# Feed-forward order by hand or by the scheduler: a two-layer sequence kernel on one Trainium2 core

## The chip, the cores and the metric

The kernel runs on one core of one Trainium2 chip. The metric is the device time of one execution in microseconds. The kernel before took 5533.02 us (median of three runs, 5531.48 to 5550.13). A core has five engines that run side by side, each through its own queue of instructions: TensorE (PE in the profile, with its weight loads as PEld), VectorE (DVE), ScalarE (ACT), GpSimd (POOL) and SyncE (SP), which here only issues DMA transfers. The kernel is written in a tile language: the program allocates tiles from pools, and a scheduler orders the instructions of each engine and sets the waits when the program is built. The order is therefore fixed before the kernel runs.

## The reference

There are two layers over x of shape (4 batches, T = 512, 128, 64), with D = 128 x 64 = 8192 features per time step. All is fp32. Cut to what matters:

```python
# layer 0
xn = layernorm(x)                                  # over D
k, v, r = xn @ Wk, xn @ Wv, sigmoid(xn @ Wr)       # D -> 64
states = scan(s = decay * s + k*v)                 # over T
x = x + (r * states) @ Wo                          # 64 -> D
x = x + gelu(conv3(layernorm(x), freq_W))          # 3 taps along the 128, 64 -> 64 channels
to = layernorm(depthwise_causal_conv3(layernorm(x)))   # 3 taps along T
x = x + to
x = x + gelu(x @ ffn_W1) @ ffn_W2                  # 64 -> 256 -> 64, for each of the 128
# layer 1
trend = moving_average(x, 25)                      # along T
x = trend + irfft(W @ rfft(x - trend)[:128])       # 128 modes, one complex 128 x 128 matrix per channel
```

## The kernel before

In layer 0 the 8192 features lie on the partitions: 64 chunks of 128 features by 512 time steps, worked on in 32 pairs of chunks (NPR = 32, NCH = 64). For each batch a generator `front` makes the first half (projections, scan, attention, convolution along the 128) and writes x2 to DRAM; a generator `back` makes the second half (norm and time convolution in a first pass, residual and feed-forward in a second). The next batch's `front` is woven into this batch's `back`: each `yield` gives a weight, and the loop at the end advances the two in proportion. Small pools decide what can lie ahead: the PSUM pools have one buffer each, the SBUF pools two or three.

The convolution part of `front` (one step for each pair of chunks):

```python
        def attend(i):
            xp = load_x(i)
            at = two(ps_a, "a")
            for j in range(2):
                js = slice(j * S, (j + 1) * S)
                nc.tensor.matmul(at[:, j, :], lhsT=wo_sb[js, i, :], rhs=rst[js, :], start=True, stop=True)   # L382
            x1 = x1s[i] = two(fr, "x1")
            nc.vector.tensor_tensor(x1, at, xp, ALU.add)
            z = zs[i] = two(fr, "z")
            # ... z[j] = x1[j] * gain * rstd, on VectorE (L388), for j in 0, 1

        def convolve(i):
            cv = two(ps_c, "c")
            # L395: two matmuls with one row of weights (-mean * rstd times the gains through the convolution)
            # L401, L405: up to four 64 x 64 matmuls with the neighbours
            # L408: two 128 x 128 matmuls
            for j in range(2):
                c = 2 * i + j
                nc.scalar.activation(cv[:, j, :], cv[:, j, :], AF.Gelu_apprx_tanh, bias=cb[:, c : c + 1])
            x2 = two(bk, "x2")
            nc.vector.tensor_tensor(x2, cv, x1s.pop(i), ALU.add)
            nc.gpsimd.dma_start(x2d[b][2 * i : 2 * i + 2].rearrange("c p t -> p c t"), x2)
            sq2 = two(bk, "sq")
            nc.scalar.activation(sq2, x2, AF.Square)
            return x2, sq2
        # ... one step later add_up (L206): four matmuls with 32 columns of ones sum x2 and x2*x2,
        #     each into its own 32 rows of one PSUM bank
```

The projections of `front` (four 128 x 128 matmuls, L279, for each pair of chunks; weights `wq` and inputs `xp` are streamed, `wq` with two buffers) and the first pass of `back` (VectorE: two products, four taps; ScalarE: two scalings, a square; a store of `to`; then L206 sums) are not touched. Below is the second pass of `back`, which is:

```python
        def residual(i):
            x2 = fetch("kx", x2d, i)
            to = fetch("kt", tod, i)
            d = two(bk, "kd")
            nc.vector.tensor_tensor(d, to, pair_of(rb), ALU.mult)
            nc.vector.tensor_tensor(d, d, pair_of(mb), ALU.subtract)
            x3 = two(bk, "k3")
            for j in range(2):
                c = slice(2 * i + j, 2 * i + j + 1)
                nc.scalar.activation(d[:, j, :], d[:, j, :], AF.Identity, bias=vec[:, B4, c], scale=vec[:, G4, c])
            nc.vector.tensor_tensor(x3, d, x2, ALU.add)
            return x3

        def widen(c, m):
            x3 = x3s[c // 2][:, c % 2, :]
            pm = two(ps_m, "m")
            for h in range(2):
                hs = slice(h * H, (h + 1) * H)
                nc.tensor.matmul(
                    pm[:, h, :], lhsT=w1_sb[hs, m * P : (m + 1) * P], rhs=x3[hs, :], start=True, stop=True
                )
            mid = mids[c, m] = bk.tile([P, 2, SL], F32, tag="mid", name="mid", bufs=3)
            nc.scalar.activation(mid, pm, AF.Gelu_apprx_tanh, bias=fb1_sb[:, m : m + 1])

        def narrow(c):
            pa = ps_p.tile([P, SL], F32, tag="p", name="pa")
            for m in range(2):
                mid = mids.pop((c, m))
                for h in range(2):
                    nc.tensor.matmul(
                        pa[h * H : (h + 1) * H, :], lhsT=w2_sb[:, m, :], rhs=mid[:, h, :],
                        start=(m == 0), stop=(m == 1),
                    )
            x4t = x4s[c] = bk.tile([P, SL], F32, tag="x4t", name="x4t")
            nc.vector.scalar_tensor_tensor(x4t, pa, fb2_sb, x3s[c // 2][:, c % 2, :], ALU.add, ALU.add)
            if c % 2:
                x3s.pop(c // 2)

        def store(c):
            x4t = x4s.pop(c)
            pt = ps_p.tile([P, NT, P], F32, tag="p", name="pt")
            for t in range(NT):
                nc.tensor.transpose(pt[:, t, :], x4t[:, t * P : (t + 1) * P], ident)
            s = c // 4
            if c % 4 == 0:
                obs[s] = bk.tile([P, NT, SL], F32, tag="ob", name="ob")
            nc.scalar.copy(obs[s][:, :, c % 4 * P : (c % 4 + 1) * P], pt)
            if c % 4 == 3:
                nc.gpsimd.dma_start(
                    x4[b][:, s * SL : (s + 1) * SL].rearrange("(t p) d -> p t d", p=P), obs.pop(s)
                )

        yield 3.0
        for c in range(NCH + 1):
            if c < NCH:
                widen(c, 0)
            if c % 2 == 0 and c // 2 + 1 < NPR:
                x3s[c // 2 + 1] = residual(c // 2 + 1)
            if c > 0:
                narrow(c - 1)
            yield BACK
            if c < NCH:
                widen(c, 1)
            if c > 0:
                store(c - 1)
            yield BACK
```

The loop that weaves the two halves, with TensorE's order set by hand (it follows the program text instead of the scheduler's choice):

```python
    whole_front = 3.5 * NPR + 12.0 + 6.0 * NPR + 6.0
    whole_back = 5.0 * (NPR + 1) + 6.0 + 2.0 * BACK * (NCH + 1)
    with tc.manual_schedule(engines={nc.tensor.engine}):
        for _ in front(0):
            pass
        for b in range(B):
            second = back(b)
            first = front(b + 1) if b + 1 < B else iter(())
            ahead = 0.0
            for weight in second:
                ahead -= weight / whole_back
                while ahead < 0.0:
                    weight = next(first, None)
                    if weight is None:
                        break
                    ahead += weight / whole_front
            for _ in first:
                pass
```

Layer 1 follows when layer 0 is done: it takes all PSUM banks, and its order is the scheduler's in both kernels.

Of the kernel before, what the change touches and what calls it, by code (L numbers as in the profile page):

```python
# [10 lines left out]
F32 = mybir.dt.float32  # L11
AF = mybir.ActivationFunctionType
ALU = mybir.AluOpType
# [3 lines left out]
P = 128  # L17
T = 512
NF = 128
H = 64  # L20
D = NF * H
NCH = D // P
SL = 512
NS = D // SL
NPR = NCH // 2
NT = T // P
# [44 lines left out]
def layer0(ctx, tc, dram, x, xt, vecs, wkvr, wo, wdec, wconv, fbias, w1, fb1, w2, fb2, x4):  # L71


    nc = tc.nc
    B = x.shape[0]
# [8 lines left out]
    bk = ctx.enter_context(tc.tile_pool(name="bk", bufs=2))  # L84
# [5 lines left out]
    ps_m = ctx.enter_context(tc.tile_pool(name="ps_m", bufs=1, space=PSUM))  # L90
    ps_p = ctx.enter_context(tc.tile_pool(name="ps_p", bufs=1, space=PSUM))

    def two(pool, tag):
        return pool.tile([P, 2, SL], F32, tag=tag, name=tag)
# [16 lines left out]
    def load(name, src):  # L111
        t = const.tile(list(src.shape), F32, name=name)
        nc.scalar.dma_start(t, src)
        return t
# [6 lines left out]
    w1_sb = load("w1_sb", w1)  # L121
    fb1_sb = load("fb1_sb", fb1)
    w2_sb = load("w2_sb", w2)
    fb2_sb = load("fb2_sb", fb2)
# [76 lines left out]
    def add_up(st, i, pair, squares, first, last):  # L201

        for j in range(2):
            for k, src in ((0, pair), (1, squares)):
                q = 2 * j + k
                nc.tensor.matmul(  # L206
                    st[32 * q : 32 * q + 32, :], lhsT=ones, rhs=src[:, j, :],
                    start=first, stop=last,
                )
# [15 lines left out]
    def moments(mean, square, tag):  # L225

        var, rs, mrs = cols(f"var{tag}"), cols(f"rs{tag}"), cols(f"mrs{tag}")
        nc.vector.tensor_tensor(var, mean, mean, ALU.mult)
        nc.vector.tensor_tensor(var, square, var, ALU.subtract)
        rsqrt(rs, var)  # L230
        nc.vector.tensor_tensor(mrs, mean, rs, ALU.mult)
        return rs, mrs
# [9 lines left out]
    def pair_of(row):  # L242
        return row.unsqueeze(1).to_broadcast([P, 2, SL])
# [189 lines left out]
        carried[b] = rows(lambda: two(ps_c, "c"), *moments(mean3, sq3, 3), "rm3")  # L433

    carried = {}
    BACK = 0.2

    def back(b):

        rb, mb = carried.pop(b)  # L440

        def fetch(tag, src, i):
            t = two(bk, tag)
            nc.sync.dma_start(t, src[b][2 * i : 2 * i + 2].rearrange("c p t -> p c t"))
            return t


        st = ps_p.tile([P, SL], F32, tag="p", name="st4")
        waiting = None
        for i in range(NPR + 1):  # L450
            if i < NPR:
                x2 = fetch("kx", x2d, i)
                xr = two(bk, "kd")
                nc.vector.tensor_tensor(xr, x2, pair_of(rb), ALU.mult)
                xh = bk.tile([P, 2, SL + 2], F32, tag="kh", name="xh")
                nc.gpsimd.memset(xh[:, :, 0:2], 0.0)
                nc.vector.tensor_tensor(xh[:, :, 2:], xr, pair_of(mb), ALU.subtract)
                to = two(bk, "k3")
                for j in range(2):
                    c = slice(2 * i + j, 2 * i + j + 1)  # L460
                    nc.scalar.activation(  # L461
                        to[:, j, :], xh[:, j, 2:], AF.Identity, bias=tb_all[:, c], scale=vec[:, W2, c]
                    )
                    for k, w in ((1, W1), (0, W0)):
                        nc.vector.scalar_tensor_tensor(  # L465
                            to[:, j, :], xh[:, j, k : SL + k], vec[:, w, c], to[:, j, :], ALU.mult, ALU.add
                        )
                cc = slice(2 * i, 2 * i + 2)
                nc.vector.tensor_tensor(to[:, :, 0:2], to[:, :, 0:2], fix[:, cc, :], ALU.add)
                nc.gpsimd.dma_start(tod[b][cc].rearrange("c p t -> p c t"), to)  # L470
                sq = two(bk, "sq")
                nc.scalar.activation(sq, to, AF.Square)
            if waiting is not None:
                n, *pair = waiting
                add_up(st, n, *pair, n == 0, n == NPR - 1)
            waiting = (i, to, sq)
            yield 5.0
        mean, sq = finish(st, lambda: two(ps_m, "m"), 4)
        rs, mrs = moments(mean, sq, 4)
        rb, mb = rows(lambda: two(ps_m, "m"), rs, mrs, "rm4")  # L480
# [14 lines that stand above are left out]
            return x3  # L495

        x3s = {0: residual(0)}
        mids, x4s, obs = {}, {}, {}

        def widen(c, m):  # L500
            x3 = x3s[c // 2][:, c % 2, :]
            pm = two(ps_m, "m")
            for h in range(2):
                hs = slice(h * H, (h + 1) * H)
                nc.tensor.matmul(  # L505
                    pm[:, h, :], lhsT=w1_sb[hs, m * P : (m + 1) * P], rhs=x3[hs, :], start=True, stop=True
                )
            mid = mids[c, m] = bk.tile([P, 2, SL], F32, tag="mid", name="mid", bufs=3)
            nc.scalar.activation(mid, pm, AF.Gelu_apprx_tanh, bias=fb1_sb[:, m : m + 1])  # L509

        def narrow(c):
            pa = ps_p.tile([P, SL], F32, tag="p", name="pa")
            for m in range(2):
                mid = mids.pop((c, m))
                for h in range(2):
                    nc.tensor.matmul(  # L516
                        pa[h * H : (h + 1) * H, :], lhsT=w2_sb[:, m, :], rhs=mid[:, h, :],
                        start=(m == 0), stop=(m == 1),
                    )
            x4t = x4s[c] = bk.tile([P, SL], F32, tag="x4t", name="x4t")  # L520
            nc.vector.scalar_tensor_tensor(x4t, pa, fb2_sb, x3s[c // 2][:, c % 2, :], ALU.add, ALU.add)  # L521
            if c % 2:
                x3s.pop(c // 2)

        def store(c):
            x4t = x4s.pop(c)
            pt = ps_p.tile([P, NT, P], F32, tag="p", name="pt")
            for t in range(NT):
                nc.tensor.transpose(pt[:, t, :], x4t[:, t * P : (t + 1) * P], ident)
            s = c // 4  # L530
            if c % 4 == 0:
                obs[s] = bk.tile([P, NT, SL], F32, tag="ob", name="ob")
            nc.scalar.copy(obs[s][:, :, c % 4 * P : (c % 4 + 1) * P], pt)  # L533
            if c % 4 == 3:
                nc.gpsimd.dma_start(
                    x4[b][:, s * SL : (s + 1) * SL].rearrange("(t p) d -> p t d", p=P), obs.pop(s)
                )

        yield 3.0
        for c in range(NCH + 1):  # L540
            if c < NCH:
                widen(c, 0)
            if c % 2 == 0 and c // 2 + 1 < NPR:
                x3s[c // 2 + 1] = residual(c // 2 + 1)
            if c > 0:
                narrow(c - 1)
            yield BACK
            if c < NCH:
                widen(c, 1)
            if c > 0:  # L550
                store(c - 1)
            yield BACK


    whole_front = 3.5 * NPR + 12.0 + 6.0 * NPR + 6.0
    whole_back = 5.0 * (NPR + 1) + 6.0 + 2.0 * BACK * (NCH + 1)
    with tc.manual_schedule(engines={nc.tensor.engine}):
        for _ in front(0):
            pass
        for b in range(B):  # L560
            second = back(b)
            first = front(b + 1) if b + 1 < B else iter(())
            ahead = 0.0
            for weight in second:
                ahead -= weight / whole_back
                while ahead < 0.0:
                    weight = next(first, None)
                    if weight is None:
                        break
                    ahead += weight / whole_front  # L570
            for _ in first:
                pass


@with_exitstack
# [184 lines left out]
```

## Time and profile before

| What | Value |
|---|---|
| time, median of three | 5533.02 us |
| span of the profiled execution | 5531.1 us |
| TensorE busy | 4819.8 us, 87% |
| VectorE busy | 2204.9 us, 40% |
| ScalarE busy | 1681.4 us, 30% |
| GpSimd busy | 338.4 us, 6% |
| DMA | 897.45 MB, mean 162 GB/s |

The profile is of one execution. For each group of instructions it gives the source line, the engine, the tiles written and read, their shapes, the count, the busy time and the mean of one, and then how long the engine stood idle just before them and what ended that wait. An fp32 matmul appears as two records. A window view gives the busy time of every engine in a stretch of the execution, and the clock that TensorE was granted (1.00 is full speed). The chain of waits follows the work back from the last instruction, at each step to what released it. "L505" is line 505 of the kernel before; in the changed kernel the same lines of layer 0's second half lie one to three lines elsewhere.

### The profile page before, as it was taken

The numbers are of one execution on the slowest core, as the hardware profiler recorded it, in microseconds if no ns is written. First come the engines' busy times: TensorE is split into PE (matmuls) and PEld (weight loads), VectorE is DVE, ScalarE is ACT, GpSimd is POOL, SyncE is SP. The second block draws the span as 40 slices with busy tenths as digits, with TensorE's granted clock in tenths as the row PEclk, the third lists the DMA queues.
The fourth block names the chain that finished last, engine by engine and source line by source line (L and its number), as shares of the span: only waits on it lengthen the run. The fifth ranks groups of instructions, "written<-read, shape, count | busy, mean of one in ns | idle before, by whom it ended". The sixth has DMA issues, their size and how long they took to land.

```text
span 5531.1 us, 43935 instructions
## 1 busy us (share of the span) xinstructions
PE 4819.8 (87%) x16675; PEld 2000.1 (36%) x16675; DVE 2204.9 (40%) x2781; ACT 1681.4 (30%) x2091; POOL 338.4 (6%) x622
## 2 busy tenths in 40 slices
PE   7788888888888888888888757788999999999999
PEld 3322332222332222332222202224844844754664
DVE  3485467544457544457544494430011111111110
ACT  0022234455324455424455455550000000000000
POOL 1100011000001000001100010000000000000000
PEclk9799999999989999999999968999999999999999
DMA  8795665434565334475433353435355345345434
GB/s 273 235 302 176 213 213 178 135 136 138 197 221 185 133 135 149 149 246 186 145 133 137 106 214 122 137 107 165 90 165 158 92 162 160 107 145 161 122 120 146
DMA packets 443830, 897.45 MB, mean 162 GB/s; under 512 B 26140, under 2 KB 92188, under 8 KB 443492
## 3 DMA queue, kind: packets, MB, share of 16 engines
q1 hardware_dynamic: 350976, 613.49, 35.1%
q0 software_dynamic: 56832, 209.74, 10.2%
q10 hardware_dynamic: 35812, 71.43, 3.4%
q8 instruction: 131, 2.15, 0.2%
q14 instruction: 79, 0.65, 0.0%
HBM read 617.70 MB, written 276.86 MB: 162 GB/s over the span
## 4 chain that ended last, share of the span: by engine, by line
PE 69%; ACT 10%; DVE 9%; DMA 8%; issue 2%; POOL 0%; SPq 0%; ACTq 0%; POOLq 0%; DVEq 0%
PE m L505 8%; PE bank L623 8%; PE bank L670 8%; PE pa L516 8%; ACT mid L509 6%; PE a L279 5%; PE st L206 4%; PE bank L642 4%; PE bank L639 4%; PE bank L668 4%; PE bank L667 4%; PE c L408 4%; PE c L401 4%; DMA wq<-wqd 3%; PE c L395 2%
## 5 line engine op out<-in xcount | busy, mean ns | idle before, releaser
L505 PE MATMUL m<-k,w_sb 64*128 64x512 f32 x2048 | 580.1, 643 | 287.6 <-ACT mid L509 279.6
L509 ACT ACTIVATE mid<-m,fb_sb 128x1024 f32<-128x1024 f32 x512 | 568.5, 1110 | 417.0 <-PE m L505 417.0
L279 PE MATMUL a<-xp,wq 128*128 128x512 f32 x1024 | 493.1, 632 | 33.2 <-DMA wq<-wqd 27.4
L516 PE MATMUL pa<-mid,w_sb 128*64 128x512 f32 x2048 | 497.7, 607 | 10.6 <-ACT ob L533 10.6
L521 DVE SCALAR_TENSOR_TENSOR x4t<-pa,fb_sb,k 128x512 f32<-128x512 f32 x256 | 192.2, 751 | 771.8 <-PE pa L516 771.6
L670 PE MATMUL bank<-yf,idft_sb 128*128 128x512 f32 x1024 | 481.4, 591 | 0.0
L623 PE MATMUL bank<-xin,dft_sb 128*128 128x512 f32 x1024 | 441.8, 594 | 16.7 <-DMA halo<-x 16.7
L465 DVE SCALAR_TENSOR_TENSOR k<-xh,vec,k 128x512 f32<-128x512 f32 x512 | 358.1, 747 | 182.8 <-ACT k L461 174.9
L605 DVE COPY ob<-bank 128x512 f32<-128x512 f32 x128 | 88.5, 692 | 789.8 <-PE bank L670 789.8
L206 PE MATMUL st<-x,ones 128*32 128x512 f32 x512 | 252.3, 645 | 142.1 <-DVE x L413 142.1
L505 PEld LDWEIGHTS m<-k,w_sb 64*128 64x128 f32 x2048 | 155.7, 185 | 574.9 <-ACT mid L509 536.0
L411 ACT ACTIVATE c<-c,cb 128x512 f32<-128x512 f32 x256 | 169.2, 661 | 616.0 <-PE c L408 612.0
L413 DVE TENSOR_TENSOR x<-c,x 128x1024 f32<-128x1024 f32 x128 | 156.5, 1223 | 439.4 <-ACT c L411 439.1
L603 ACT COPY ob<-bank 128x512 f32<-128x512 f32 x128 | 75.0, 586 | 804.8 <-PE bank L670 804.8
L206 PE MATMUL st<-sq,ones 128*32 128x512 f32 x1024 | 306.5, 678 | 4.9
L279 PEld LDWEIGHTS a<-xp,wq 128*128 128x128 f32 x1024 | 198.0, 201 | 304.4 <-issue 281.1
L642 PE MATMUL bank<-xf,w 128*128 128x128 f32 x1024 | 304.3, 397 | 0.0
L639 PE MATMUL bank<-xf,w 128*128 128x128 f32 x1024 | 304.1, 397 | 0.0
L623 PEld LDWEIGHTS bank<-xin,dft_sb 128*128 128x128 f32 x1024 | 195.1, 191 | 262.3 <-issue 262.3
L670 PEld LDWEIGHTS bank<-yf,idft_sb 128*128 128x128 f32 x1024 | 192.9, 188 | 246.9 <-issue 246.9
L493 ACT ACTIVATE kd<-kd,vec 128x512 f32<-128x512 f32 x256 | 203.8, 807 | 248.9 <-DVE kd L489 248.9
L461 ACT ACTIVATE k<-xh,tb_all,vec 128x512 f32<-128x512 f32 x256 | 194.0, 804 | 255.1 <-PE st L206 174.6
(155 smaller groups left out, 5836.5 us busy)
## 6 DMA issues: line engine op xcount, KB each, us to landing
xp<-in_xt SPq DMA_DIRECT2D x256, 512.0 KB
kx<-x SPq DMA_DIRECT2D x256, 512.0 KB
xin<-x SPq DMA_DIRECT2D x128, 1024.0 KB
xk<-in_x SPq DMA_DIRECT2D x64, 1024.0 KB
x<-x POOLq DMA_DIRECT2D x128, 512.0 KB, 3.6
to<-k POOLq DMA_DIRECT2D x128, 512.0 KB, 3.8
kt<-to SPq DMA_DIRECT2D x128, 512.0 KB
x<-ob POOLq DMA_DIRECT2D x64, 1024.0 KB, 7.8
```

The costliest lines, as they stand in the source:

```text
L206: nc.tensor.matmul(st[32 * q : 32 * q + 32, :], lhsT=ones, rhs=src[:, j, :], start=first, stop=last,)
L279: nc.tensor.matmul(pa[:, k, :], lhsT=wq[:, j, k * P : (k + 1) * P], rhs=xp[:, j, :], start=first and j == 0, stop=last and j == 1,)
L401: nc.tensor.matmul(cv[0:H, j, :], lhsT=wc_sb[H:P, P:], rhs=prev[H:P, :], start=False, stop=False)
L408: nc.tensor.matmul(cv[:, j, :], lhsT=wc_sb[:, 0:P], rhs=z[:, j, :], start=False, stop=True)
L465: nc.vector.scalar_tensor_tensor(to[:, j, :], xh[:, j, k : SL + k], vec[:, w, c], to[:, j, :], ALU.mult, ALU.add)
L505: nc.tensor.matmul(pm[:, h, :], lhsT=w1_sb[hs, m * P : (m + 1) * P], rhs=x3[hs, :], start=True, stop=True)
L509: nc.scalar.activation(mid, pm, AF.Gelu_apprx_tanh, bias=fb1_sb[:, m : m + 1])
L516: nc.tensor.matmul(pa[h * H : (h + 1) * H, :], lhsT=w2_sb[:, m, :], rhs=mid[:, h, :], start=(m == 0), stop=(m == 1),)
L623: nc.tensor.matmul(pf, lhsT=dft_sb[:, k, r, :], rhs=xin[:, k, :], start=(k == 0), stop=(k == NT - 1))
L639: nc.tensor.matmul(o, lhsT=w[:, j, r, :], rhs=xf[:, 0, :, c], start=True, stop=False)
L642: nc.tensor.matmul(o, lhsT=w[:, j, 2 if r == 0 else 0, :], rhs=xf[:, 1, :, c], start=False, stop=True,)
L670: nc.tensor.matmul(po, lhsT=idft_sb[:, r, kk], rhs=yff[:, r, c], start=False, stop=(r == 1))
```

## The change

The feed-forward pass is written as one plain loop, and TensorE's order is left to the scheduler. Three things go: the hand-set order of TensorE, the functions that let the widening of one chunk run ahead of the narrowing of the chunk before it, and the small weights (0.2) that placed most of the next batch's `front` beside the first pass of `back`. In their place stand weights of 2, 2, 2 and 1 for each chunk. No arithmetic changes, and the pools and the transfers stay as they are. The stated purpose is a first layer with features on the partitions throughout, streamed over pairs of chunks from DRAM to DRAM; both kernels have that, so what differs is only the order.

```diff
@@ -433,7 +433,6 @@
         carried[b] = rows(lambda: two(ps_c, "c"), *moments(mean3, sq3, 3), "rm3")
 
     carried = {}
-    BACK = 0.2
 
     def back(b):
 
@@ -495,81 +494,65 @@
             return x3
 
         x3s = {0: residual(0)}
-        mids, x4s, obs = {}, {}, {}
-
-        def widen(c, m):
+        ob = None
+        yield 3.0
+        for c in range(NCH):
             x3 = x3s[c // 2][:, c % 2, :]
-            pm = two(ps_m, "m")
-            for h in range(2):
-                hs = slice(h * H, (h + 1) * H)
-                nc.tensor.matmul(
-                    pm[:, h, :], lhsT=w1_sb[hs, m * P : (m + 1) * P], rhs=x3[hs, :], start=True, stop=True
-                )
-            mid = mids[c, m] = bk.tile([P, 2, SL], F32, tag="mid", name="mid", bufs=3)
-            nc.scalar.activation(mid, pm, AF.Gelu_apprx_tanh, bias=fb1_sb[:, m : m + 1])
-
-        def narrow(c):
+            mids = []
+            for m in range(2):
+                pm = two(ps_m, "m")
+                for h in range(2):
+                    hs = slice(h * H, (h + 1) * H)
+                    nc.tensor.matmul(
+                        pm[:, h, :], lhsT=w1_sb[hs, m * P : (m + 1) * P], rhs=x3[hs, :], start=True, stop=True
+                    )
+                mid = bk.tile([P, 2, SL], F32, tag="mid", name="mid", bufs=3)
+                nc.scalar.activation(mid, pm, AF.Gelu_apprx_tanh, bias=fb1_sb[:, m : m + 1])
+                mids.append(mid)
+                yield 2.0
+            if c % 2 == 0 and c // 2 + 1 < NPR:
+                x3s[c // 2 + 1] = residual(c // 2 + 1)
             pa = ps_p.tile([P, SL], F32, tag="p", name="pa")
             for m in range(2):
-                mid = mids.pop((c, m))
                 for h in range(2):
                     nc.tensor.matmul(
-                        pa[h * H : (h + 1) * H, :], lhsT=w2_sb[:, m, :], rhs=mid[:, h, :],
+                        pa[h * H : (h + 1) * H, :], lhsT=w2_sb[:, m, :], rhs=mids[m][:, h, :],
                         start=(m == 0), stop=(m == 1),
                     )
-            x4t = x4s[c] = bk.tile([P, SL], F32, tag="x4t", name="x4t")
-            nc.vector.scalar_tensor_tensor(x4t, pa, fb2_sb, x3s[c // 2][:, c % 2, :], ALU.add, ALU.add)
-            if c % 2:
-                x3s.pop(c // 2)
-
-        def store(c):
-            x4t = x4s.pop(c)
+            x4t = bk.tile([P, SL], F32, tag="x4t", name="x4t")
+            nc.vector.scalar_tensor_tensor(x4t, pa, fb2_sb, x3, ALU.add, ALU.add)
+            yield 2.0
             pt = ps_p.tile([P, NT, P], F32, tag="p", name="pt")
             for t in range(NT):
                 nc.tensor.transpose(pt[:, t, :], x4t[:, t * P : (t + 1) * P], ident)
-            s = c // 4
             if c % 4 == 0:
-                obs[s] = bk.tile([P, NT, SL], F32, tag="ob", name="ob")
-            nc.scalar.copy(obs[s][:, :, c % 4 * P : (c % 4 + 1) * P], pt)
+                ob = bk.tile([P, NT, SL], F32, tag="ob", name="ob")
+            nc.scalar.copy(ob[:, :, c % 4 * P : (c % 4 + 1) * P], pt)
             if c % 4 == 3:
-                nc.gpsimd.dma_start(
-                    x4[b][:, s * SL : (s + 1) * SL].rearrange("(t p) d -> p t d", p=P), obs.pop(s)
-                )
-
-        yield 3.0
-        for c in range(NCH + 1):
-            if c < NCH:
-                widen(c, 0)
-            if c % 2 == 0 and c // 2 + 1 < NPR:
-                x3s[c // 2 + 1] = residual(c // 2 + 1)
-            if c > 0:
-                narrow(c - 1)
-            yield BACK
-            if c < NCH:
-                widen(c, 1)
-            if c > 0:
-                store(c - 1)
-            yield BACK
+                s = c // 4
+                nc.gpsimd.dma_start(x4[b][:, s * SL : (s + 1) * SL].rearrange("(t p) d -> p t d", p=P), ob)
+            if c % 2:
+                x3s.pop(c // 2)
+            yield 1.0
 
 
     whole_front = 3.5 * NPR + 12.0 + 6.0 * NPR + 6.0
-    whole_back = 5.0 * (NPR + 1) + 6.0 + 2.0 * BACK * (NCH + 1)
-    with tc.manual_schedule(engines={nc.tensor.engine}):
-        for _ in front(0):
+    whole_back = 5.0 * (NPR + 1) + 6.0 + 7.0 * NCH
+    for _ in front(0):
+        pass
+    for b in range(B):
+        second = back(b)
+        first = front(b + 1) if b + 1 < B else iter(())
+        ahead = 0.0
+        for weight in second:
+            ahead -= weight / whole_back
+            while ahead < 0.0:
+                weight = next(first, None)
+                if weight is None:
+                    break
+                ahead += weight / whole_front
+        for _ in first:
             pass
-        for b in range(B):
-            second = back(b)
-            first = front(b + 1) if b + 1 < B else iter(())
-            ahead = 0.0
-            for weight in second:
-                ahead -= weight / whole_back
-                while ahead < 0.0:
-                    weight = next(first, None)
-                    if weight is None:
-                        break
-                    ahead += weight / whole_front
-            for _ in first:
-                pass
 
 
 @with_exitstack
```

## The prediction

> **What bounds the kernel now.** I read the page first (shares, slices, chain), then a table of windows by stage, then three short stretches of the timeline.
>
> ```profile
> PE 4819.8 (87%) x16675; PEld 2000.1 (36%) x16675; DVE 2204.9 (40%) x2781; ACT 1681.4 (30%) x2091; POOL 338.4 (6%) x622
> ...
> PE 69%; ACT 10%; DVE 9%; DMA 8%; issue 2%; POOL 0%; SPq 0%; ACTq 0%; POOLq 0%; DVEq 0%
> ...
> L505 PE MATMUL m<-k,w_sb 64*128 64x512 f32 x2048 | 580.1, 643 | 287.6 <-ACT mid L509 279.6
> L206 PE MATMUL st<-x,ones 128*32 128x512 f32 x512 | 252.3, 645 | 142.1 <-DVE x L413 142.1
> ```
>
> TensorE is busy 87% and holds 69% of the chain that ended last. Its 711 us of idle time have two large owners: the widening matmul (L505) waiting for GELU (L509), 280 us, and the sums (L206) waiting for VectorE. TensorE's order is just what the change leaves to the scheduler.
>
> ```profile
> 606.00:770.00 164.00, 144.29 (x424) 59.72 (x424) 99.56 (x138) 45.80 (x53) 17.00 (x37) 0.94 0.79 275
> 794.00:1013.00 219.00, 191.93 (x737) 48.23 (x734) 150.03 (x184) 83.95 (x107) 28.80 (x52) 0.98 0.51 168
> 1033.00:1455.00 422.00, 349.25 (x1493) 111.76 (x1491) 179.42 (x181) 232.77 (x275) 19.20 (x26) 1.00 0.37 128
> ...
> 3161.00:3338.00 177.00, 94.98 (x280) 16.25 (x280) 162.39 (x228) 83.91 (x98) 27.74 (x65) 0.68 0.56 201
> 3350.00:3750.00 400.00, 303.59 (x1280) 97.02 (x1278) 158.73 (x155) 215.39 (x252) 12.15 (x16) 0.97 0.37 123
> 3754.00:4195.00 441.00, 440.81 (x1273) 250.68 (x1274) 43.68 (x64) 36.92 (x63) 11.23 (x18) 1.00 0.44 138
> ```
>
> Columns: window, length, busy PE, PEld, DVE, ACT, POOL (instructions), PE clock, DMA share, GB/s. The kernel is front of batch 0 alone (0 to 606 us), three like periods of about 850 us (606 to 1455, 1455 to 2308, 2308 to 3161), batch 3's back half alone (3161 to 3750), and layer 1 (3754 to the end, four times 442 us, TensorE full). A period is a **first part** of 427 us (k/v/r projections, back's norm pass, 26 of the next batch's 32 convolution steps) and a **feed-forward part** of 422 us with only 6 steps in it. In the first row the DMA is 79% busy; in the fourth, VectorE 92%.
>
> ```profile
> 1057.92 1.13 PE L505 MATMUL m<-k,w_sb 64*128 64x512 f32 x4 [0.69 <-ACT mid L509]
> 1058.97 1.94 PE L516 MATMUL pa<-mid,w_sb 128*64 128x512 f32 x8
> 1060.84 1.13 PE L505 MATMUL m<-k,w_sb 64*128 64x512 f32 x4
> 1061.90 0.65 PE L529 MATMUL pt<-ident,x4t 128*128 128x128 f32 x4
> ...
> 852.19 1.05 PE L206 MATMUL st<-x,ones 128*32 128x512 f32 x2 [0.71 <-DVE x L413]
> 853.31 0.62 PE L206 MATMUL st<-sq,ones 128*32 128x512 f32 x1
> ...
> 854.30 1.13 PE L395 MATMUL c<-rm,cgr 1*128 1x512 f32 x4
> ```
>
> An fp32 matmul shows as two records. Start to start, a widening pair costs 1.06 us (1057.92 to 1058.97), the four narrowing matmuls 1.87 us, the four transposes about 0.75. The last three lines are what the change multiplies: one sum alone holds TensorE as long (1.05 us) as the other three together (853.31 to 854.30, 0.99 us), since those lie in different columns of the array and run at once.
>
> **What the Trainium skill says.** "TensorEngine Tiling (Array Packing)", Key Properties: "Changing tiling mode (not just tile) drains the TensorE", and tiles work in parallel. The trace agrees: four half-width sums take the time of one, and each change of line costs about 0.15 us over its streaming time (1.87 us for four slots of 0.43). "TensorE: Matmul & The Clock Gate", Step-by-step, says that matmuls stay in program order and only weight loads are pulled ahead; the L505 waits with ready work behind them agree. The same page, on the clock gate, says an idle TensorE is slowed; the clock of 0.68 in the norm pass alone against 1.00 in the feed-forward part agrees.
>
> **The change part by part.** The arithmetic is the same: 8852 TensorE instructions before and after, by the built programs, whose orders are fixed before any run. Front 0 and layer 1 keep their order but for details. Four things move.
>
> (1) *Weights of the interleave.* The feed-forward part weighs 7.0 x 64 = 448 instead of 0.2 x 130 = 26. So the projections now run with the norm pass alone, and all 32 convolution steps go into the feed-forward part.
>
> (2) *First part, new.* The norm pass alone took 177 us (row 3161:3338), VectorE-bound at 10.25 us per two steps (a chain of VectorE taps and the 5 us store of its result). Now 25 MB of projection loads lie beside it: two steps move 3.67 MB, which in 10.25 us would be 358 GB/s, where the stretch 606 to 770 sustained 275 at a share of 0.79. TensorE has 8 x 0.87 + 3.1 + switches, 10.3 us, as well. I take 12.5 us: 16 x 12.5 = 200, plus 12 to start, 212. The end of the sums, residual 0 and the state scan of the next batch now lie together: 26 us (before, 20 to 25 us each at 770 and 1013). First part: **238 us**, 189 less than 427.
>
> (3) *Feed-forward part, new.* TensorE's work with all groups whole: per chunk 2 x 1.06 + 1.87 + 0.75 = 4.74 us, x 64 = 303 (the trace has 303.6); per convolution step 0.98 (L382) + 1.05 (L395) + 1.86 (L401, L405) + 1.91 (L408) + 1.05 (L206) = 6.85, x 32 = 219; together 522. But the scheduler cuts groups up. I counted the stretches in the built order of this part: L395 stands alone 50 times (25 lost pairs), L382 24 times (12 pairs), the sums split 1 and 3 in 27 steps of 32, and 106 half-groups of narrowing. With each lone matmul at 1.0 to 1.05 us: widening 136, narrowing 125, transposes 46, L382 43, L395 57, L401/L405 62, L408 61, sums 60, in all 591. That is 69 us of lost packing. Next, one dense step laid out by hand: 18.5 us of TensorE, VectorE 9.1 (1.22 + 1.41 + 1.23 for the step, 3.68 + 1.50 for two chunks) and ScalarE 9.6. I find one stall of about 0.6 us per step, at the second widening pair, where GELU stands behind the convolution's two GELUs in ScalarE's queue. 32 x 0.6 = 19, plus some start: **615 us**, 193 more than 422.
>
> So a period goes from 849 to 853 us. Put in another way: TensorE's idle time falls from 129 (849 less 720 busy) to 92 us (68 in the first part, where its own work is 170, and 24 in the second), while its work grows from 720 to 761 (+69 for lost packing, less 27 since the 26 steps in the old first part already paid for the sum of x2 alone). Three periods: +12 us.
>
> (4) *Feed-forward of batch 3 alone.* Before, order by hand: widen, narrow the chunk before, widen, store. The trace repeats in 11.94 us per two chunks (L505 starts at 3501.35 and 3513.29). The new order is widen, transpose, widen, narrow *the same* chunk. Laid out with the same durations (first pair 1.06, GELU 1.11 with 0.18 ahead and 0.06 behind): odd chunk 5.75 us, because the second half of narrowing waits out the second GELU. In the even chunk two ScalarE scalings surround that GELU, and the first waits for VectorE (x4t, x3, two products: 4.7 us after narrowing ends), so it takes 7.6 us. 13.35 per two chunks against 11.94: 32 x 1.41 = **+45 us**.
>
> Sum: 5533 + 12 + 45 = 5590. I add 20, since the hand layout of (3) supposes that VectorE and ScalarE come in time everywhere: **5610 us**.
>
> **The rivals.** *Filling wins*: the convolution steps fill every GELU wait and lone matmuls overlap their neighbours on free rows or columns. For it: the 280 us of L505 waits and engines half empty in that part. Against: a narrowing or transposing neighbour takes all rows. If packing cost half of 69 us, a period is 35 us shorter, total 5505. *The in-order engines collide*: TensorE's finer interleave makes it wait on VectorE or ScalarE instructions stuck behind others, as ScalarE's L493 already does here. For it: two streams share single PSUM buffers. Against: the same schedule orders all engines. At 10% idle in that part a period is 45 us longer: 5745. *The DMA takes the first part*: the weight loads queue on SyncE behind loads that wait for VectorE. At 15 us per two steps, +40 a period, 5730; were the norm pass undisturbed, 35 less, 5505.
>
> **Range and chances.** Each rival is worth about 100 us either way, part (4) about 20. Low 5500, high 5730. The line at plus 2% is 5644, at minus 2% 5422. Faster 0.07, within 0.53, slower 0.40.
>
> **What would show it.** The first part (first projection to first widening matmul) 220 to 260 us with DMA share 0.8 or more; the feed-forward part 600 to 640 us with TensorE over 95% busy; L382 and L395 with a higher total busy time than now; the L505 waits on GELU cut to under 130 us, most of them in batch 3; that part 430 to 450 us from its first widening matmul to its last store, not 395. I am wrong if a period differs from 850 us by over 40, if the feed-forward part has TensorE under 90%, or if front 0 or layer 1 moves by over 10 us.

## The result and the profile after

| | before | after |
|---|---|---|
| time, median of four | 5532.33 us (5531.48 to 5550.13) | 5575.32 us (5570.81 to 5582.84) |
| ratio, 95% interval | 1 | 1.0071 [1.0048, 1.0095] |
| span of the profiled execution | 5531.1 us | 5571.3 us |

The changed kernel is 0.7% slower: 43 us by the medians, 40 us by the two profiled spans. The page of the changed kernel has these lines in place of those shown of before (shares by engine, the chain, two groups):

```profile
PE 5094.9 (91%) x16675; PEld 2025.8 (36%) x16675; DVE 2185.8 (39%) x2781; ACT 1687.9 (30%) x2091; POOL 337.3 (6%) x622
...
PE 35%; DVE 4%; ACT 2%; DMA 1%; issue 1%; SPq 0%; POOL 0%; ACTq 0%; DVEq 0%; POOLq 0%
...
L506 PE MATMUL m<-k,w_sb 64*128 64x512 f32 x2048 | 604.6, 649 | 85.5 <-ACT mid L510 78.0
L518 PE MATMUL pa<-mid,w_sb 128*64 128x512 f32 x2048 | 552.8, 623 | 71.5 <-ACT mid L510 71.5
```

With the same 16675 records TensorE is busy 275 us longer, and its idle time has fallen from 711 to 476 us. The wait of the widening matmul for GELU (L505 before, L506 now) went from 280 to 78 us, but the narrowing matmul (L518) now waits 72 us for the same GELU, almost all of it in batch 3 (67). The chain breaks off early in this trace (its shares sum to 43%), so I don't use it. The stages say more; the windows of the changed kernel (columns as before: window, length, busy PE, PEld, DVE, ACT, POOL, clock, DMA share, GB/s):

```profile
220.00:668.00 448.00, 378.88 (x948) 98.86 (x948) 238.30 (x339) 82.00 (x102) 27.33 (x38) 0.80 0.54 178
...
887.00:1501.00 614.00, 594.96 (x2184) 173.53 (x2184) 277.06 (x291) 290.45 (x350) 35.73 (x49) 0.98 0.39 132
1501.00:1695.00 194.00, 177.71 (x570) 57.44 (x566) 166.88 (x235) 86.74 (x102) 28.23 (x67) 0.99 0.88 314
1714.00:2327.00 613.00, 593.95 (x2178) 172.62 (x2178) 276.54 (x287) 290.31 (x350) 35.74 (x49) 0.98 0.39 132
...
3347.00:3790.00 443.00, 317.94 (x1276) 91.97 (x1276) 153.82 (x151) 213.37 (x250) 12.15 (x16) 0.97 0.32 108
```

The rows are the convolution steps of front 0, a feed-forward part, a first part, the next feed-forward part, and batch 3's feed-forward alone. The same row of before for front 0 is

```profile
220.00:604.00 384.00, 304.71 (x979) 86.29 (x978) 238.74 (x346) 83.09 (x103) 29.48 (x39) 0.89 0.65 214
```

A stage of sums ends here where TensorE starts on the matmuls (L217) that read the finished sums (L206). With these ends the 40 us split like this:

| Stage | before, us | after, us | difference |
|---|---|---|---|
| front 0 (start to the end of its sums) | 603.7 | 668.1 | +64.4 |
| three periods | 2554.5 | 2484.0 | -70.5 |
| norm pass of batch 3 | 176.9 | 175.0 | -1.9 |
| feed-forward of batch 3, to layer 1 | 419.1 | 466.8 | +47.7 |
| layer 1 | 1776.9 | 1777.4 | +0.5 |

So the small number hides three large ones. In a period (the second of the three) TensorE's busy time rose from 722 to 782 us and its idle time fell from 131 to 44; front 0 and the last batch's feed-forward gave more than that gain back.

### The profile page after: what moved, and what is told of

It reads as the page before. It is cut to its first block, busy times and chain, and to the rows that moved or that the text cites. A ratio compares the mean times of both kernels' runs of the same rounds, so it can differ in the third digit from the quotient of the medians.

```text
span 5571.3 us, 43812 instructions
## 1 busy us (share of the span) xinstructions
PE 5094.9 (91%) x16675; PEld 2025.8 (36%) x16675; DVE 2185.8 (39%) x2781; ACT 1687.9 (30%) x2091; POOL 337.3 (6%) x622
## 5 line engine op out<-in xcount | busy, mean ns | idle before, releaser
L506 PE MATMUL m<-k,w_sb 64*128 64x512 f32 x2048 | 604.6, 649 | 85.5 <-ACT mid L510 78.0
L518 PE MATMUL pa<-mid,w_sb 128*64 128x512 f32 x2048 | 552.8, 623 | 71.5 <-ACT mid L510 71.5
L279 PE MATMUL a<-xp,wq 128*128 128x512 f32 x1024 | 511.5, 634 | 34.5 <-DMA wq<-wqd 33.6
L206 PE MATMUL st<-x,ones 128*32 128x512 f32 x512 | 268.4, 639 | 59.5 <-DVE x L413 59.5
L206 PE MATMUL st<-k,ones 128*32 128x512 f32 x512 | 238.0, 699 | 91.6 <-DVE k L468 91.6
L506 PEld LDWEIGHTS m<-k,w_sb 64*128 64x128 f32 x2048 | 164.6, 187 | 421.0 <-issue 232.0
L206 PE MATMUL st<-sq,ones 128*32 128x512 f32 x1024 | 308.9, 682 | 1.3 <-ACT sq L471 0.4
L279 PEld LDWEIGHTS a<-xp,wq 128*128 128x128 f32 x1024 | 186.1, 197 | 331.8 <-issue 310.9
L401 PE MATMUL c<-z,wc_sb 64*64 64x512 f32 x504 | 288.8, 696 | 0.0
L405 PE MATMUL c<-z,wc_sb 64*64 64x512 f32 x504 | 288.2, 695 | 0.4 <-DVE z L388 0.3
```

What stands on the lines that cost most here:

```text
L206: nc.tensor.matmul(st[32 * q : 32 * q + 32, :], lhsT=ones, rhs=src[:, j, :], start=first, stop=last,)
L279: nc.tensor.matmul(pa[:, k, :], lhsT=wq[:, j, k * P : (k + 1) * P], rhs=xp[:, j, :], start=first and j == 0, stop=last and j == 1,)
L401: nc.tensor.matmul(cv[0:H, j, :], lhsT=wc_sb[H:P, P:], rhs=prev[H:P, :], start=False, stop=False)
L405: nc.tensor.matmul(cv[H:P, j, :], lhsT=wc_sb[0:H, P:], rhs=after[0:H, :], start=False, stop=False)
L506: nc.tensor.matmul(pm[:, h, :], lhsT=w1_sb[hs, m * P : (m + 1) * P], rhs=x3[hs, :], start=True, stop=True)
L518: nc.tensor.matmul(pa[h * H : (h + 1) * H, :], lhsT=w2_sb[:, m, :], rhs=mids[m][:, h, :], start=(m == 0), stop=(m == 1),)
```

## The experiments

The theory after the result had four parts. (a) Front 0 is longer because the scheduler breaks up packed groups of matmuls there, and the clock falls as a consequence. (b) The periods are shorter because the convolution steps are spread over the feed-forward part, not because of the scheduler's order. (c) That order costs about 69 us of lost packing per period. (d) Batch 3 is longer because each chunk's narrowing waits out its own GELU. The rivals: front 0 waits for transfers or VectorE; the scheduler's own interleave makes the gain; the DMA sets the length of a period; batch 3 lacks a PSUM buffer, whatever the order.

### Front 0 by hand, and with its pairs whole

Two kernels, each the changed one with an edit to front 0. The first sets TensorE's order there by hand again; the second leaves it to the scheduler but for one edge per step, so that a step's convolution is issued after the sums of the step before.

```diff
-    for _ in front(0):
-        pass
+    with tc.manual_schedule(engines={nc.tensor.engine}):
+        for _ in front(0):
+            pass
```

> The changed kernel with TensorE's program order kept in front 0 alone. Theory 1 (the 64 us that front 0 lost, 604 to 668 us, come from TensorE's order alone: the two one-row matmuls L395 apart, and the slower clock that follows): front 0 ends near 604 us, a convolution step takes 9.7 us again, total 5511 us (5500 to 5525). Rival (front 0 lost because VectorE's statistics L288 and the loads of xk stand elsewhere in the queues): front 0 stays above 640 us, total 5555 to 5575.

```diff
-                waiting = (i - 1, *convolve(i - 1))
+                if b == 0 and i > 1:
+                    with tc.issue_after(added[0].ins):      # added[0]: the last of the four sums
+                        waiting = (i - 1, *convolve(i - 1))
```

> The changed kernel with one edge per step in front 0: the convolution's matmuls are issued after the step's four sums, so that the pair L395 stays whole; attention stays one step further ahead, and everything else is the scheduler's. Theory 1a (the broken pair alone is the cause, with the clock that it drags down): as with the hand order, front 0 ends at 604 to 615 us, total 5510 to 5525. Rival (attention running one step ahead makes VectorE's z wait for the convolution and holds up the queue): front 0 stays above 640 us, total over 5550.

By hand: 5512.58 us, 0.9933 [0.9913, 0.9954] of before; front 0 ends at 594.9 us. With the edge alone: 5515.75 us, 0.9947 [0.9932, 0.9963]; front 0 ends at 613.2. What the edge does is seen in one step. The timeline of TensorE in the changed kernel:

```profile
570.01 1.05 PE L206 MATMUL st<-x,ones 128*32 128x512 f32 x2 [1.70 <-DVE x L413]
570.99 1.12 PE L395 MATMUL c<-rm,cgr 1*128 1x512 f32 x2
...
573.57 2.07 PE L395 MATMUL c<-rm,cgr 1*128 1x512 f32 x2
575.57 1.11 PE L401 MATMUL c<-z,wc_sb 64*64 64x512 f32 x1
...
579.18 2.00 PE L408 MATMUL c<-z,wc_sb 128*128 128x512 f32 x4
```

and in the kernel before:

```profile
546.27 1.04 PE L206 MATMUL st<-x,ones 128*32 128x512 f32 x2 [1.71 <-DVE x L413]
...
548.35 1.13 PE L395 MATMUL c<-rm,cgr 1*128 1x512 f32 x4
549.41 0.64 PE L401 MATMUL c<-z,wc_sb 64*64 64x512 f32 x1
```

Before, the two L395 matmuls (one row of weights each, in different row groups) are one group of four records and take 1.06 us, start to start. After, the scheduler puts one L395 between the first sum, which stands alone in both kernels, and the other three: two records at a time, twice the price. Besides, the middle of the step runs at half the clock (from 572.4 to 579.2 us in the trace's record of the clock): 2.07 us for what took 1.12, and 1.11 for a record that took 0.64. Before, 18 of 31 steps were 9.75 us long; after, none was, and they took 10.7 to 15.6. With the edits 9.75 is again the commonest length (18 steps by hand, 13 with the edge), so (a) holds and a wait for a transfer does not: none was removed. What separates 613 from 595 is likely scatter for the most part: the first profile is of the fastest of four executions (5496.38 us), the second of the slowest of ten (5534.61), while the medians differ by 3 us. In all profiles of this case front 0 ended at 594 to 609 us with TensorE's order by hand and whole groups, and at 668 to 686 in the changed kernel and the three below that leave front 0 as it is there.

### The same break made by hand, and then filled

Does the break alone do this, or something else in the scheduler's order? The first kernel of this pair takes front 0 by hand and moves one L395 matmul between the first sum and the other three. The second adds to that two full matmuls per step, whose result nobody reads, so that TensorE is not idle there. The edits are cut to what matters.

```diff
                 nc.tensor.matmul(st[32 * q : 32 * q + 32, :], lhsT=ones, rhs=src[:, j, :], ...)
+                if between is not None and q == 0:
+                    between()                               # the first L395 matmul of the next step
```

> The run with front 0 by hand, but in front 0 the pair L395 is broken by hand just as the scheduler broke it: one of the two stands between the first sum and the other three. Theory 1 (broken pair and slower clock make the 64 us): steps of 13 to 14 us where nothing else holds them, front 0 ends at 655 to 670 us, total 5560 to 5580. Rival (the broken pair costs only its own 1 us a step, and the rest of the loss came from elsewhere): front 0 ends at 620 to 630 us, total 5530.

```diff
+            if b == 0:
+                spare = two(ps_m, "m")
+                for j in range(2):
+                    nc.tensor.matmul(spare[:, j, :], lhsT=wc_sb[:, 0:P], rhs=decb, start=True, stop=True)
```

> The run with the pair L395 broken in front 0, and two full matmuls more per step (64 in all, into a PSUM tile that nobody reads, 1.7 us a step) in the gap between attention and the first sum, where TensorE idles 1.7 us. Theory 1 (the step is long because the granted clock drops when TensorE idles and then works on lone narrow matmuls): more work makes front 0 shorter; full clock, steps of 10.7 to 11.2 us, front 0 at 610 to 635 us, total 30 to 55 us below the broken run. Rival (the step is long by its chain of waits alone): front 0 as long as in the broken run or up to 60 us longer.

Broken: 5583.43 us, 1.0096 [1.0073, 1.0119], just above what was expected; front 0 ends at 673.9. Broken and filled: 5538.55 us, 1.0010 [1.0001, 1.0020]; front 0 ends at 628.3. The same 87 us of front 0 in the kernel with front 0 by hand, in the broken one and in the filled one:

```profile
505.00:592.00 87.00, 69.22 (x221) 17.21 (x220) 28.85 (x30) 21.21 (x27) 6.41 (x9) 0.94 0.28 91
```

```profile
505.00:592.00 87.00, 75.05 (x187) 18.14 (x186) 27.06 (x32) 16.66 (x21) 5.08 (x7) 0.81 0.23 76
```

```profile
505.00:592.00 87.00, 87.00 (x249) 24.02 (x250) 30.17 (x32) 18.08 (x23) 5.82 (x8) 0.96 0.30 97
```

The order of one matmul is enough: the clock falls from 0.94 to 0.81 and fewer records get done (187 against 221). With *more* work in every step the clock is back at 0.96 and front 0 is 45 us shorter. A lost pair alone can cost at most 32 steps x 1.05 us = 34 us; broken against whole, front 0 is 79 us longer (673.9 against 594.9), so about 45 us is the clock. The steps show it one by one: in the broken kernel 12 of 31 take 10.68 us with every record at full speed, which puts the lost pair at 0.93 us a step; the other 19 take 13.9 to 17.2 us, with records at half speed.

"TensorE: Matmul & The Clock Gate" of the Trainium skill, in "HAM oscillation — how this bites in real kernels", gives the rule as no idle gaps of TensorE over about 3.4 us. Here the only gap worth naming in the step, before the first sum, is 1.71 us in the kernel before and 1.70 in the changed one; one had a clock of 0.97 in these 87 us and the other 0.83. So keeping gaps below that length is not enough. Nor is it idle time alone: in the filled kernel TensorE is busy for all of the 87 us, and still every third step takes 12.47 us instead of 10.82, with the same matmul (L401 before, L419 in this kernel) slow in the one and fast in the next:

```profile
533.03 1.05 PE L419 MATMUL c<-z,wc_sb 64*64 64x512 f32 x1
...
545.46 0.59 PE L419 MATMUL c<-z,wc_sb 64*64 64x512 f32 x1
```

What the filling shows is that more work in the step raises the clock. Whether it counts how much of the array a matmul uses was not tried.

### Spreading the convolution, with the order by hand

The kernel before with one number changed: the weight of each half chunk of feed-forward, first 3.5, which gives that part the weight that the change gives it (2 x 3.5 x 65 = 455 against 448), then 2.2.

```diff
-    BACK = 0.2
+    BACK = 3.5    # in the second kernel 2.2
```

> The kernel before with the weight of a feed-forward half chunk 3.5 instead of 0.2: the convolution steps are spread over the feed-forward as in the changed kernel, but TensorE's order is by hand and every group stays whole. Theory 1 (spreading is worth about 70 us a period, and the scheduler's order gives most of it back through lone matmuls): periods of about 800 us instead of 849, total 5390 us (5330 to 5440). Rival (spreading itself is worth no more than the 23 us a period that the changed kernel shows, as in-order waits take the rest in any order): periods of 825 us or more, total 5460 to 5535.

> The kernel before with the weight of a feed-forward half chunk 2.2 (3.5 in the run before, 0.2 in the kernel before): all 32 projection steps now fit into the first part, and only the convolution steps lie beside the feed-forward. Theory 1 (TensorE's own work in whole groups, 522 us, bounds the feed-forward part, plus some 50 us of waits): first part 215 us, feed-forward part 580 us, periods of about 795 us, total 5360 us (5330 to 5400). Rival (waits in program order grow as the convolution steps stand closer together): no better than weight 3.5, total 5420 or more.

With 3.5: 5433.58 us, 0.9798 [0.9780, 0.9815], periods of 815 to 819 us (about 800 expected). With 2.2: 5372.28 us, 0.9715 [0.9692, 0.9738], periods of 797 to 803. So the weights alone make the gain, and more of it than the change did (826). Packing is whole here. In the changed kernel's second feed-forward part and in this one's (3.5), 128 records of L395 stand in the groups by line, after and then by hand:

```profile
L395 PE MATMUL c<-rm,cgr 1*128 1x512 f32 x128 | 64.0, 640 | 0.0
```

```profile
L395 PE MATMUL c<-rm,cgr 1*128 1x512 f32 x128 | 37.0, 655 | 0.0
```

Count and mean are equal, yet the busy time, which counts overlapping matmuls once, differs by 27 us: that is how lost packing shows in a profile. But not all of it is gained. From the end of the norm pass's sums to the end of the period, TensorE is busy 44 us less than in the changed kernel (561 against 605), with 26 us of the next batch's projections in it besides; yet this stretch is only 18 us shorter (614 against 632). By hand, TensorE waits: 54 us there instead of 27. The widening group of the same part with 3.5:

```profile
L505 PE MATMUL m<-k,w_sb 64*128 64x512 f32 x512 | 145.0, 640 | 36.4 <-ACT mid L509 32.4 <-DVE k L494 4.0
```

A convolution step comes in two lumps, attention and then sums and convolution, so that every other half chunk has none, and there widening waits for GELU as before.

### The convolution in four pieces

So the lumps were cut at the borders of its packed groups: attention; the sums of the step before and the L395 pair; the neighbours; the middle. One piece goes into each half chunk.

```diff
+            yield 1.5          # in convolve, after the L395 pair, and again after L401 and L405
-                waiting = (i - 1, *convolve(i - 1))
-            yield 3.0
+                waiting = (i - 1, *(yield from convolve(i - 1)))
+            yield 1.5
-    BACK = 0.2
+    BACK = 2.2
```

> As the run with weight 2.2, and each convolution step is cut by hand into four pieces of whole groups (L382; L206 and L395; L401 and L405; L408), one for each feed-forward half chunk, so that between any two widening pairs there is always a piece. Theory 1 (what is left in the hand order is the wait of L505 for GELU where no convolution group stands between): waits of L505 under 20 us a period, periods of 775 to 785 us, total 5310 us (5270 to 5350). Rival (the pieces delay the feed-forward chain and add drains, so nothing is gained): within 15 us of the run with weight 2.2.

5213.20 us, 0.9427 [0.9405, 0.9448]; every period is 747 to 748 us, better than expected. A period of the changed kernel and one of this kernel:

```profile
1501.00:2327.00 826.00, 782.14 (x2790) 238.54 (x2788) 454.20 (x537) 383.14 (x459) 66.07 (x118) 0.98 0.50 173
```

```profile
1344.00:2092.00 748.00, 702.29 (x2792) 233.19 (x2788) 456.06 (x537) 381.53 (x458) 65.58 (x118) 0.97 0.55 191
```

The widening group in this kernel's feed-forward part:

```profile
L507 PE MATMUL m<-k,w_sb 64*128 64x512 f32 x512 | 143.4, 637 | 9.8 <-DVE k L496 7.4 <-ACT mid L511 2.3
```

TensorE's idle time in the period is 46 us, close to the scheduler's 44, and its busy time 702 us against 782: 80 us. With as many records, and idle time and clock (0.97 and 0.98) nearly equal, what is left between the two orders is packing, so (c) holds. (In the kernel with 2.2, whose groups are whole too and whose clock was 0.96 and 0.97, TensorE is busy 715 and 707 us in the second and third period. So the size is 67 to 80.) The first part of this kernel is 197 us, that of the changed one 194, both with the DMA at a share of 0.88: the DMA did not set the length of the period, which fell by 78 us beside it.

### The scheduler's order with the small weights

The fourth corner: the changed kernel with its weights scaled so that the feed-forward part counts as little as before (0.4 a chunk instead of 7).

```diff
-                yield 2.0
+                yield 2.0 * SMALL      # SMALL = 0.4 / 7; likewise at the other two yields and in whole_back
```

> The changed kernel (scheduler's order) with the small weights of before (0.4 a chunk instead of 7): the other corner of order by weight. Theory 1 (order and weight act apart; the scheduler's order costs 64 us in front 0, 48 us at the end, and breaks 29 of 32 L395 pairs a period now in the first part; the spread of the convolution steps was the gain of the change): periods of 880 to 925 us, total 5720 to 5850. Rival (the weights do nothing of themselves, a period in the scheduler's order is 828 us either way): total 5560 to 5600.

5807.23 us, 1.0483 [1.0437, 1.0530]. With the four corners side by side, the second and third period take ("the scheduler's order" includes the plain loop here):

| | small weights | large weights |
|---|---|---|
| order by hand | 853 us | 817 us |
| the scheduler's order | 901 us | 826 us |

The weights gain 36 us by hand and 75 with the scheduler; the scheduler costs 48 us with small weights and 9 with large ones. The change combined a good half with a bad one. Part of the 48 us may be the clock, which was 0.93 and 0.94 in these two periods against 0.97 before. L395 is busy 322.7 us in all here, 283.0 in the changed kernel and 151.9 before, for the same 512 records.

### The last batch's feed-forward

Two edits to batch 3, where no convolution is left: the old loop with TensorE by hand, and the changed loop with a second PSUM tile, so that the second widening need not wait until GELU has emptied the first.

```diff
+        if b == B - 1:
+            # the old loop: widen(c, 0), narrow(c - 1), widen(c, 1), store(c - 1)
+            with tc.manual_schedule(engines={nc.tensor.engine}):
```

> The changed kernel with the old feed-forward program and TensorE's program order for batch 3 alone, the one that has nothing beside it. Theory 1 (narrowing right behind its own second widening makes TensorE wait out the GELU): the part from 3327 us to the end of layer 0 goes from 467 to 419 us, total 5527 us (5518 to 5537). Rival (the part is longer because of its late first chunks and its last store): under 20 us gained, total over 5555.

```diff
-                pm = two(ps_m, "m")
+                pm = two(ps_a, "a") if b == B - 1 and m else two(ps_m, "m")
```

> The changed kernel, in batch 3's feed-forward alone the second widening of each chunk goes to the PSUM tile of the attention, which is free there. The scheduler now also breaks the widening pairs and half-groups. Theory 1 (lone matmuls cost a full turn each): GELU waits go, but four lone matmuls a pair of chunks take their place; 430 to 450 us from the start of the feed-forward to the end of layer 0 against 467, total 5540 to 5560. Rival (only the GELU wait counts, packing does not): 350 to 380 us, total 5465 to 5490.

By hand: 5534.63 us, 0.9985 [0.9974, 0.9995]; the stage takes 417 us instead of 467, so (d) holds. With the second tile: 5537.74 us, 0.9999 [0.9987, 1.0012], 420 us (430 to 450 expected). The buffer recovers as much as the old order, with no gain over it. The changed kernel's timeline shows the waits that I had laid out:

```profile
3502.32 1.08 PE L518 MATMUL pa<-mid,w_sb 128*64 128x512 f32 x4 [2.07 <-ACT mid L510]
3503.33 1.13 PE L506 MATMUL m<-k,w_sb 64*128 64x512 f32 x4
3505.73 1.13 PE L506 MATMUL m<-k,w_sb 64*128 64x512 f32 x4 [0.69 <-ACT mid L510]
3506.79 1.08 PE L518 MATMUL pa<-mid,w_sb 128*64 128x512 f32 x4
3508.13 1.08 PE L518 MATMUL pa<-mid,w_sb 128*64 128x512 f32 x4 [0.27 <-ACT mid L510]
3509.14 1.13 PE L506 MATMUL m<-k,w_sb 64*128 64x512 f32 x4
```

One chunk runs from 3503.33 to the next first widening at 3509.14, 5.81 us. With the second tile the widening is no longer one packed group of four records:

```profile
3500.61 1.12 PE L506 MATMUL m<-k,w_sb 64*128 64x512 f32 x2
3501.67 1.08 PE L518 MATMUL pa<-mid,w_sb 128*64 128x512 f32 x4
```

Here the scheduler uses the new freedom to put a half group of widening ahead of a half group of narrowing; TensorE is busy 383 us of 418, where the changed kernel had 318 of 443. The waits went, and lost packing took their place.

### Both together

The kernel with four pieces, and the second tile for batch 3, order by hand:

> The run with four pieces, and in batch 3's feed-forward the same second PSUM tile, with the order by hand. Theory 1 (whole groups, no GELU wait: TensorE's 303 us bound it): 320 to 345 us instead of 417 from the end of the norm pass to the end of layer 0, total 5125 to 5145. Rival (VectorE and ScalarE in order hold it: the L493 wait): 380 us or more, total 5175 or more.

5145.98 us, 0.9287 [0.9254, 0.9320], the best of all, 7.1% under the kernel before. Batch 3's feed-forward:

```profile
3029.00:3378.00 349.00, 307.23 (x1305) 102.76 (x1305) 165.75 (x164) 216.27 (x258) 13.39 (x18) 0.95 0.44 148
```

349 us, a little over what was expected. The tile that recovered 47 us with the scheduler is worth 68 by hand (417 to 349): TensorE's busy time stays at 307 us, as the packed groups give it. So batch 3 did lack a PSUM buffer, in either order; that does not take anything from (d), since the old order recovered 50 us without one.

## Why the prediction was right, and where it was not

5610 was predicted and 5575 measured, inside the range and inside "within 2%". That the sum came out so near is partly luck: front 0 was 64 us longer than forecast and the periods 83 us shorter, and the two errors offset each other.

- **Front 0: wrong.** "Front 0 and layer 1 keep their order but for details" is the step that failed. Layer 1 stayed (+0.5 us), but one of the details was the L395 pair of every step, and it cost 64 us. I had counted the lone L395 matmuls of the feed-forward part and did not count those of front 0 in the same built order; and I had not thought of the clock. The condition that I gave for being wrong, front 0 moving by over 10 us, came true.
- **First part: too long in the sum.** 238 us were predicted, 219 and about 212 measured (in the first and the second period). Both terms were too large: two steps took 11.4 us in the mean of the second period (9.9 to 12.8), not 12.5, since the DMA carried 314 GB/s at a share of 0.88 where I had taken 275 at 0.79 as a guide to the limit; and the transition took 18 to 19 us, not 26. That makes most of the periods' miss: -70.5 us instead of +12, and the "undisturbed" side of the DMA rival was nearer than my middle.
- **Feed-forward part: right, by its mechanism.** 615 us were predicted and 614, 613 and 612 measured; TensorE's work 591 predicted (its rounded terms add up to 590) and 593 to 595 measured, so it is 97% busy. The lost packing of 69 us, counted in the built order before any run, is 67 to 80 us against two kernels with whole groups. Reading the order for lone members of packed groups, as "TensorEngine Tiling (Array Packing)" of the Trainium skill, Key Properties, gives reason to (tiles work in parallel), carried the prediction. (The sums that it calls half-width use 32 of the array's 128 columns.) The waits of L505 fell to 78 us, under the 130 stated, with 48 of them in batch 3; that L518 would wait 72 us in their place is in the layout of part (4), but I had not named it as a sign.
- **Batch 3: right.** +45 predicted, +47.7 measured; 437 us from its first widening to its last store (430 to 450 predicted), an odd chunk of 5.81 us against 5.75. By hand it went back by 50 us.
- **The 20 us added for collisions: no ground.** The feed-forward part met its number without them. The rival in which the in-order engines collide did not come true; the rival in which filling wins came true for the idle time (131 to 44 us in a period) but not for the packing.

## What to carry to other kernels

Where small matmuls are packed side by side in the array, read the built order for members that stand alone: each costs as much as its whole group, and the profile shows it only as busy time that grows at equal count and mean, which looks like better use of the engine. When one stream is to fill another's waits, cut it at the borders of its packed groups and put one piece into each wait; here that was worth 5.7%, and 7.1% with a second PSUM tile, where the change as it was made lost 0.7%. After a change of order look at the clock column of every stage, also of those that were not meant to change.

## What the runs showed of the hardware that was not expected

- Two more full matmuls in every step of front 0 made it 45 us shorter (673.9 to 628.3 us), with the clock at 0.96 instead of 0.81.
- The clock fell inside steps of 14 us in which TensorE's only idle gap was 1.70 us, as long as in the steps of 9.75 us before; a one-row matmul took 1.12 us at the start of the step and its twin, 2.6 us later, 2.07. With no idle gap at all, in the filled kernel, the clock still fell in every third step.
- Transfers beside the norm pass ran at 314 GB/s in the second period, at a share of 0.88, where the kernel before had shown 275 at 0.79.
